# A transformer layer on one core: reordering the first projection, the key and query loads, and the merging of one attention unit

## The chip, the core and the metric

The kernel runs on one core of a Trainium2 chip. The core has a matrix engine (PE; its weight loads are listed apart as PEld), a vector engine (DVE), a scalar engine for activations and copies (ACT), a general engine (POOL), and an engine that issues transfers (SP). Every engine works through its own queue in order and waits on semaphores for the others. The metric is device time in microseconds (us) for one execution; lower is better.

## The reference

Two sequences of 1024 tokens, 512 wide, in float32, go through one post-norm layer. LoRA means that each weight gets half of a rank-16 product added.

```python
q, k, v = (split_heads(lora_linear(x, ...)) for each of q, k, v)      # 16 heads of 32
attn = softmax(q @ k.T * 32 ** -0.5)
x = layernorm(x + lora_linear(merge_heads(attn @ v), Wo, bo, Bo, Ao))
probs = softmax(x @ Wg); expert = argmax(probs); gate = max(probs)    # 8 experts, 256 slots each
routed = gate * ((silu(xe @ W1) * (xe @ W3)) @ W2)                    # 0 for tokens beyond the slots
shared = (silu(x @ sw1) * (x @ sw3)) @ sw2
x = layernorm(x + routed + shared)
```

## The kernel before

Most products are made of two halves. A value is split into a high part, rounded to the fast matrix format, and the low rest; a product is then high·high + low·high + high·low.

**First projection** (lines 216 to 430). Tokens come in four blocks `tb` of 512, weights in four chunks `k` of 128 rows. For block 0 and the query weight the loop at lines 395 to 400 runs over `k`, and `proj_all` (389) calls `proj_k` (306) for each of the four head groups: three matmuls, weight high with token high, weight high with token low, weight low with token high. `split_w` folds the LoRA product into a raw weight chunk (DVE, L284) and splits it (ACT L285 high, DVE L289 low). `split_xk` splits the tokens (ACT L299 high; for block 0 POOL makes the low part, L300). This first part has a written order for ACT, DVE and POOL too; after it only PE's order is written, and a planner places the rest of the projection on the other engines. `split_lora` prepares the LoRA factors of one weight; `prep_w(1, r1)` does it for the key weight after chunk 1. Queries and keys go to DRAM.

**Attention** (lines 587 to 810) has 16 units `u`: one batch, one group `g = u // 2` of four heads, one half of the queries. A unit has 8 steps, one for each block of 128 keys, so step `t = 8u + k`. All engines' orders are written out. In step `t`, `st_step` makes scores for four heads (PE L608) and exponentials (ACT L617) into probability tiles `pt` (two of 128x1024 a step, one for each pair of heads, from a ring of 14). Functions hung into `between[0..3]` run after each of the four heads: `av_step(t-1)` multiplies with the values (PE L635); `adds` sums the probability tiles over the key blocks of a unit; `s1_step` works 12 steps ahead (`LEAD`) on row maxima of a later unit (PE L187, DVE L195), so it ends at step 115; `finish_max` transposes the maxima and hands them to the query tile (`mp`, `mh`, `ml`, L205 to L211).

The sums: POOL adds (L627), except that tile 1 of a unit is added to tile 2 by an accumulating DMA that POOL issues (L655; in unit 13 tiles 1 and 6). In units 14 and 15, DVE and POOL share the adds (`DVE_END`): in unit 14 nine are on DVE and five on POOL, in unit 15 seven and five. `finish(u)` multiplies the sums with ones (PE L670) and, for units 13 to 15, inverts on DVE (L680). `normalize(u)` multiplies (DVE L709), rounds (ACT L711) and takes the rest (DVE L713). In unit 14 it works on unit 13 at its step 7 (t = 119), and in unit 15 on unit 14 at its step 4 (t = 124); `finish(14)` is in step 122.

**Loads.** At `k == 0` of an even unit, SP issues `load_k` for the later half of the next group's keys, three transfers of 256 KB, and `load_q` for unit u+2, three more. `load_k` for the first half is issued at `k == 6` of the odd unit before. `load_res` fetches a residual row block at `RES_AT` (step 8i+6 for the first eight), and POOL adds a bias to it three steps later (`add_res`, L722).

**After it**: the output projection (`oproj`, L739; the first block of batch 1 begins in steps 126 and 127, `OPROJ1`), the list `TAIL`, and the shared experts, 8 blocks `st` of 6 chunks `c`. `SCHED` hangs into (st, c) the preparing of a later block (`p`, transposes), its router logits (`a`: `logits_a`) and their transposition (`b`). `p` and `a` and `b` share two PSUM banks. Then come the router, the scatter and the eight experts.

Of the kernel before, what the change touches and what calls it, by code (L numbers as in the profile page):

```python
# [2 lines left out]

# [10 lines left out]
ALU = mybir.AluOpType  # L14
# [4 lines left out]
P = 128  # L19
B, L, D = 2, 1024, 512  # L20
NU = 16
T = B * L
NH, HD = 16, 32
NG = 4
KC = D // P
# [7 lines left out]
LEAD = 12  # L33
LATE, OP_ONE = (0,), 1
NS = NU * 8
# [21 lines left out]
NRM = 0  # L57
K_AT = 6
XTB = 5
ON_DVE = ()  # L60
ON_DMA = {NU - 3: (1, 6)}
ADDS = {0: (0,), 2: (1,), 3: (3,), 4: (4,), 5: (2,), 6: (5,), 7: (6,)}
ADDS_END = {0: (0,), 2: (1,), 3: (3,), 4: (4,), 5: (2,), 7: (6, 5)}
OPROJ_AT = (65, 67, 69, 71, 73, 75, 77, 79)
RES_AT = tuple(8 * i + 6 for i in range(8)) + (70, 78, 86, 94, 98, 102, 106, 110)
RES_ADDS = tuple(t + 3 for t in RES_AT[:14]) + (118, 119)
RB = 2
BTB = 4
AHEAD = 5
# [1 line left out]
W2_AT = {2: (0, 1), 3: (2, 3), 4: (4,), 5: (5,)}  # L71
MPJ, MPP = 0, 2
RDIR = NU - 3
FINE, NRME = 2, {NU - 2: 7, NU - 1: 4}
DVE_END = {
    NU - 2: ((1, 0), (7, 0)) + tuple((i, 1) for i in range(1, 8)),
    NU - 1: ((1, 0), (2, 0), (3, 0), (4, 0), (5, 0), (6, 0), (6, 1)),
}
OPROJ1 = -2
ROOT_LAG, NORM_LAG = 1, 4  # L80
HSB = 8
TAIL = (
# [3 lines left out]
SCHED = {  # L86
# [4 lines left out]
}  # L91
W13 = 5 * 1024 + 512
# [5 lines left out]
def kernel(  # L98
# [5 lines left out]
    def f(ap):  # L104
        return ap.bitcast(F32)
# [33 lines left out]
    qk_d = {}  # L139
# [4 lines left out]
                    qk_d[w, b, g, hl] = dram.tile([P, L], F32, name=f"qkd{w}{b}{g}{hl}")  # L144
    v_d = [dram.tile([L, D], F32, name=f"vd{b}") for b in range(B)]

    def load_k(g, cs=slice(0, 1024)):
        kt = Ks[g % 2]
        for blk, hl in ((0, 0), (1, 1), (2, 0)):
            sp.dma_start(  # L150
                out=f(kt[32 * blk : 32 * blk + 32, :, cs]),
                in_=qk_d[1, g // NG, g % NG, hl].rearrange("(h p) t -> p h t", p=32)[:, :, cs],
            )

    def load_v(g):
# [8 lines left out]
            ],  # L164
        )

    def load_q(u):
        g, qb = u // 2, u % 2
        for blk, hl in ((0, 0), (1, 0), (2, 1)):
            sp.dma_start(  # L170
                out=f(Qs[u % 3][32 * blk : 32 * blk + 32]),
                in_=qk_d[0, g // NG, g % NG, hl].rearrange("(h p) t -> p h t", p=32)[
                    :, :, qb * 512 : qb * 512 + 512
                ],
            )

# [41 lines left out]
    with ExitStack() as ph1, tc.manual_schedule(engines=MAN1):  # L218
# [33 lines left out]
            return raws  # L252


        def prep_w(i, raws):
            ba = split_lora(i, raws)
            for k, lp in enumerate([fold_w(i, ba, k) for k in range(KC)]):
                split_w(i, k, raws, lp)

        def split_lora(i, raws):  # L260
            ba = []
            for j, lo in ((0, 64), (1, 32)):
                t_ = sg.tile([LR, D], F32R, name=f"lora{i}{j}", tag=f"lora{j}", bufs=1)
                act.copy(t_, raws[j])
                rows = slice(lo, lo + R)
                dve.tensor_tensor(t_[rows], raws[j][rows], f(t_[rows]), ALU.subtract)
                ba.append(t_)
            return ba
# [40 lines left out]
        def proj_k(o, xs, w, g, k):  # L309
            hi, lo = xs[k]  # L310
            a = wh[w][:, k, g * P : g * P + P]
            c = wl[w][:, k, g * P : g * P + P]
            for i, (lhs, rhs) in enumerate(((a, hi), (a, lo), (c, hi))):
                pe.matmul(o, lhs, rhs, start=k + i == 0, stop=k + i == KC + 1)  # L314
# [61 lines left out]
        with tc.manual_schedule(engines=MAN0):  # L376
            dve.memset(bo_bc, 0.0)
            warm("hot", WARM)
            ba = split_lora(0, r0)
            lps = [fold_w(0, ba, k) for k in range(KC)]  # L380
            warm("warm", 1)
            os_ = [bank1(f"o00{g}") for g in range(NG)]
            xs = []

            def split_k(k):
                split_w(0, k, r0, lps[k])
                xs.append(split_xk(0, k, x0[k]))

            def proj_all(k):
                for g in range(NG):  # L390
                    proj_k(os_[g], xs, 0, g, k)

            pool.memset(f(Ks[0][96:98, :, :]), -1.0)
            for k in range(KC):
                split_k(k)
            pool.memset(f(Ks[1][96:98, :, :]), -1.0)
        for k in range(KC):
            proj_all(k)
            if k == KC - 3:
                prep_w(1, r1)  # L400
        for tb in range(4):
            if tb == 0:
                for g in range(NG):
# [23 lines left out]
            xs = xn  # L427
# [161 lines left out]
    with ph2, tc.manual_schedule(engines={mybir.EngineType.PE}):  # L589
# [28 lines left out]
                for fn in between[h]:  # L618
                    fn()

        def add_step(t, pr):
            u, kc = t // 8, t % 8
            if kc == 0:
                accs[u, pr] = pts[t, pr]
            elif kc not in direct(u):
                eng = dve if (kc, pr) in DVE_END.get(u, ON_DVE) else pool
                eng.tensor_tensor(accs[u, pr], accs[u, pr], pts[t, pr], ALU.add)  # L627

        def av_step(t):
            u, kc = t // 8, t % 8  # L630
            g = u // 2
# [9 lines left out]
                    skip_group_check=True,  # L641
                )

        def adds(t):
            u, kc = t // 8, t % 8
            if u in DVE_END:
                for pr in range(2):
                    add_step(t, pr)  # L650
                return
            for j, pr in product((ADDS_END if u in ON_DMA else ADDS).get(kc, ()), range(2)):
                i = u * 8 + j
                if j in ON_DMA.get(u, (1,)):
                    pool.dma_start(out=pts[i + 1, pr], in_=pts[i, pr], accum_op=ALU.add)  # L655
                else:
                    add_step(i, pr)

        def direct(u):
            return () if u in NO_DIR else DIRECT  # L660
# [43 lines left out]
        def normalize(u, parts=(0, 1, 2)):  # L704
            g, qb = u // 2, u % 2
            cs = slice(qb * 512, qb * 512 + 512)
            hi, lo = at_h[:, g % NG, cs], at_l[:, g % NG, cs]
            if 0 in parts:
                dve.tensor_tensor(avs[u], avs[u], fin[u], ALU.mult)  # L709
            if 1 in parts:  # L710
                act.copy(hi, avs[u])  # L711
            if 2 in parts:
                dve.tensor_tensor(lo, avs[u], f(hi), ALU.subtract)  # L713

# [44 lines left out]
        for t in range(NS):  # L759
            u, k = t // 8, t % 8  # L760
            if k == 0:
                if u % 2 == 0 and 2 <= u and u // 2 + 1 < B * NG:
                    load_k(u // 2 + 1, slice(512, 1024))
                if u >= 1 and u + 2 < NU:
                    load_q(u + 2)
                if u % 2 and NG <= u // 2 + 1 < B * NG:
                    load_v(u // 2 + 1)

            if k == K_AT and u % 2 and u // 2 + 2 < B * NG:
                load_k(u // 2 + 2, slice(0, 512))  # L770
            if t in RES_AT:
                load_res(RES_AT.index(t))
            between = [[], [], [], []]
            if t + LEAD < NS:
                for q in range(4):
                    between[q].append(lambda q=q: s1_step(t + LEAD, q))
            elif t + LEAD == NS:
                between[0].append(lambda: finish_max(NU - 1))
            if t:
                between[1].append(lambda: av_step(t - 1))  # L780
                if t == NS - LEAD - 1:

                    between[3].append(lambda: (adds(t - 2), adds(t - 1)))
                elif t != NS - LEAD - 2:
                    between[1].append(lambda: adds(t - 1))
                if u and k == (FINE if u == NU - 1 else FIN):
                    between[1 if u == NU - 1 else FINQ].append(lambda: finish(u - 1))
            if u:
                for v in [u - 2] * (k == NRM and 1 < u < NU - 1) + [u - 1] * (k == NRME.get(u)):
                    between[0].append(lambda v=v: normalize(v, (0,)))  # L790
                    between[1].append(lambda v=v: normalize(v, (1,)))
                    between[2].append(lambda v=v: normalize(v, (2,)))
# [477 lines left out]
```

## Time and profile before

| what | us |
|---|---|
| median of 3 runs (lowest, highest) | 1061.65 (1058.94, 1062.08) |
| the profiled execution | 1072.63 |
| its span, first to last instruction | 1070.8 |

The profiled execution is 10.98 us longer than the median of the runs. Busy time of PE in its stretches, from the view by windows:

| stretch (us) | PE busy (us) | what runs there |
|---|---|---|
| 0 to 60 | 55.55 | first projection, beginning |
| 180 to 250 | 68.15 | attention, first units |
| 450 to 500 | 50.00 | attention |
| 550 to 600 | 45.00 | attention, units 13 to 15 |
| 650 to 700 | 48.81 | shared experts |
| 750 to 800 | 42.66 | router, scatter |
| 900 to 1000 | 100.00 | experts |
| 1000 to 1071 | 58.28 | experts, end |

How to read the views: a group line gives source line, engine, operation, output <- inputs, count, busy time and mean, then the idle time before it and what ended it. A line of the view of waits gives who waited, for whom, the sum in us, how often, and the longest. A timeline line gives start, duration, engine, line, operation and count, and in brackets the idle time before. A line by windows gives for each engine busy time and count, then PE's granted clock, the DMA engines' busy share and GB/s.

### The profile page before, as it was taken

Reading aid. Unit: us, or ns where it says so; the run is one execution under the profiler, and the core shown is the slowest. Engines: PE = TensorE matmul, PEld = TensorE weight load, DVE = VectorE, ACT = ScalarE, POOL = GpSimd, SP = SyncE. Lnnn points to the kernel's source line nnn. Section 1 sums busy time; section 2 is a strip of 40 time slices with the busy share of each in tenths; the row PEclk is TensorE's granted clock in tenths of the full one; section 3 lists DMA queues with packets and bytes.
Section 4 is the critical chain, followed back from the end, with each engine's and each line's share of the span. In section 5 each row is a group of like instructions: output and inputs, shape, how many; then the busy total and the mean of one; then the engine's idle time right before and its main releaser. Section 6 shows DMA issues by size and latency. Waiting matters only on the chain. (4 is left out here: it accounts for less than half of the span.)

```text
span 1070.8 us, 16471 instructions
## 1 busy us (share of the span) xinstructions
PE 1033.8 (97%) x5994; PEld 744.5 (70%) x5994; DVE 697.2 (65%) x1190; ACT 529.2 (49%) x1025; POOL 596.1 (56%) x406
## 2 busy tenths in 40 slices
PE   8999999999999999999998999999979999999995
PEld 6888774444444455544443379899959999999994
DVE  6732788778787877778789974224412567777752
ACT  5422216666666655566665745223102446655552
POOL 4000006999999986979997764000230036766674
PEclk9999999999999999999999999999989999999998
DMA  9876863364637462645643031000280356777721
GB/s 281 280 225 204 250 195 94 78 142 95 143 82 148 115 133 70 131 97 119 143 110 80 1 109 60 21 21 21 92 243 31 118 171 225 254 255 246 258 79 59
DMA packets 84008, 146.68 MB, mean 137 GB/s; under 512 B 14756, under 2 KB 23460, under 8 KB 83928
## 3 DMA queue, kind: packets, MB, share of 16 engines
q1 hardware_dynamic: 75768, 117.30, 37.5%
q0 software_dynamic: 8160, 28.33, 10.7%
q8 instruction: 47, 0.77, 0.3%
q14 instruction: 33, 0.27, 0.1%
HBM read 95.83 MB, written 33.78 MB: 121 GB/s over the span
## 5 line engine op out<-in xcount | busy, mean ns | idle before, releaser
L195 DVE TENSOR_REDUCE mt<-s 128x1 f32<-128x512 f32 x512 | 324.0, 682 | 83.3 <-PE s L187 82.8
L627 POOL TENSOR_TENSOR pt<-pt,pt 128x1024 f32<-128x1024 f32 x148 | 362.0, 2909 | 11.3 <-ACT pt L617 10.8
L617 ACT ACTIVATE pt<-st 128x512 f32<-128x512 f32 x512 | 269.8, 601 | 135.0 <-PE st L608 120.4
L608 PE MATMUL st<-qs,ks 98*128 98x512 f32 x512 | 214.1, 428 | 3.3 <-DVE ml L209 2.1
L187 PE MATMUL s<-ks,qs 96*128 96x512 f32 x512 | 200.3, 398 | 5.3 <-DMA qs<-qkd 4.2
L608 PEld LDWEIGHTS st<-qs,ks 98*128 98x128 f32 x512 | 95.9, 189 | 135.8 <-issue 93.9
L884 PE MATMUL h<-xthe,w13s 128*128 128x256 f32 x704 | 129.9, 283 | 0.0
L872 POOL TENSOR_TENSOR w2s<-w2r,w2s 128x512 fp32r<-128x512 f32 x42 | 65.9, 1590 | 107.4 <-ACT w2s L871 107.2
L655 POOL DMA_DIRECT2D pt<-pt x30 | 27.4, 1078 | 170.5 <-PE st L608 170.5
L187 PEld LDWEIGHTS s<-ks,qs 96*128 96x128 f32 x512 | 97.0, 189 | 26.1 <-DVE mt L195 6.5
L884 PEld LDWEIGHTS h<-xthe,w13s 128*128 128x128 f32 x704 | 110.7, 191 | 0.3
L884 PE MATMUL h<-xtle,w13s 128*128 128x256 f32 x352 | 100.2, 285 | 0.0
L635 PE MATMUL av<-pt,vt 128*32 128x512 f32 x512 | 75.8, 612 | 1.9 <-ACT pt L617 1.9
L1032 POOL DMA_INDIRECT xd_d<-x1a,slot_i x8 | 7.9, 986 | 111.6 <-DVE slot_i L1029 109.5
L635 PE MATMUL av<-pt,x1b 128*32 128x512 f32 x512 | 68.2, 605 | 0.0
L884 PEld LDWEIGHTS h<-xtle,w13s 128*128 128x128 f32 x352 | 67.4, 191 | 0.7
L928 PE MATMUL y<-w2s,hs 128*128 128x512 f32 x260 | 60.9, 390 | 0.1
L928 PEld LDWEIGHTS y<-w2s,hs 128*128 128x128 f32 x260 | 48.2, 188 | 10.2 <-DVE hs L910 0.5
L314 PE MATMUL o<-xh,wh 128*128 128x512 f32 x128 | 50.6, 395 | 1.7 <-ACT xh L299 1.0
L314 PE MATMUL o<-xl,wh 128*128 128x512 f32 x128 | 50.9, 397 | 0.9 <-POOL xl L300 0.9
L329 ACT ACTIVATE oh<-o,bqk_sb 128x512 fp32r<-128x512 f32 x32 | 21.9, 688 | 57.9 <-PE o L314 54.5
L314 PE MATMUL o<-xh,wl 128*128 128x512 f32 x128 | 50.4, 394 | 0.0
(823 smaller groups left out, 1810.9 us busy)
## 6 DMA issues: line engine op xcount, KB each, us to landing
pt<-pt POOLq DMA_DIRECT2D x30, 512.0 KB
qs<-qkd SPq DMA_DIRECT2D x48, 256.0 KB
x1a<-in_w_dram SPq DMA_DIRECT2D x24, 512.0 KB
w2r<-in_w_dram SPq DMA_DIRECT2D x42, 256.0 KB
ks<-qkd SPq DMA_DIRECT2D x36, 256.0 KB
qkd<-oh SPq DMA_DIRECT2D x32, 256.0 KB
qkd<-ol SPq DMA_DIRECT2D x32, 256.0 KB
x1b<-in_w_dram SPq DMA_DIRECT2D x16, 512.0 KB
```

What stands on the lines that cost most here:

```text
L187: pe.matmul(s1, Qs[u % 3][0:96, h, qt * P : qt * P + P], Ks[g % 2][0:96, h, kh * 512 : kh * 512 + 512], start=True, stop=True,)
L195: dve.tensor_reduce(mts[u][:, c, kh : kh + 1], s1, AX.X, ALU.max)
L314: pe.matmul(o, lhs, rhs, start=k + i == 0, stop=k + i == KC + 1)
L329: act.activation(oh, o, AF.Identity, bias=bias)
L608: pe.matmul(sb, Ks[g % 2][:, h, kc * P : kc * P + P], Qs[u % 3][:, h, :], start=True, stop=True,)
L617: act.activation(pts[t, h // 2][:, h % 2, :], sb, AF.Exp, scale=SCALE)
L627: eng.tensor_tensor(accs[u, pr], accs[u, pr], pts[t, pr], ALU.add)
L635: pe.matmul(avs[u][32 * h : 32 * h + 32, :], vts[g][:, kc, 32 * h : 32 * h + 32], pts[t, h // 2][:, h % 2, :], start=kc == 0, stop=kc == 7 ...
L655: pool.dma_start(out=pts[i + 1, pr], in_=pts[i, pr], accum_op=ALU.add)
L872: pool.tensor_tensor(hl[:, 1, :], raw, f(hl[:, 0, :]), ALU.subtract)
L884: pe.matmul(hp[:, j * 256 : j * 256 + 256], lhs, rhs[:, k, :], start=n == 0, stop=n == 11,)
L928: pe.matmul(o, lhs, rhs, start=n == 0, stop=n == 16)
```

## The change

1. The query projection of token block 0: for chunks 0 to 2, four groups with weight high and token high, then four with weight low and token high, then four with token low. `split_lora(1)` is written between the splits of chunk 1 and chunk 2.
2. At `k == 0` of an even unit the three key and three query transfers become two rounds of three and three, each with two of the four heads (128 KB each). Odd units load queries as before.
3. `load_res` of the odd blocks moves to step 8i+2 (and likewise 74 and 90 in the second half; 98 becomes 100), `add_res` three steps later.
4. Unit 14: tiles 0, 2, 4 are added to tiles 1, 3, 5 by DMA (two each, for the two pairs of heads), tiles 3, 6, 7 and 5 to tile 1 by DVE (eight adds), in steps 119 and 120; POOL adds none. Unit 15 keeps its split. `finish(14)` moves to step 123, `normalize(13)` to step 118, `normalize(14)` to step 125, with the rounding and the rest behind the fourth head. For units 13 and 14 the rounding is on DVE instead of ACT.
5. The first block of the output projection of batch 1 no longer begins in steps 126 and 127.
6. `a5` moves from (1, 5) to (2, 0).

```diff
+ADDS = {
+    None: {0: "bb0", 2: "dd1", 3: "pp3", 4: "pp4", 5: "pp2", 6: "pp5", 7: "pp6"},
+    NU - 3: {0: "bb0", 2: "dd1", 3: "pp3", 4: "pp4", 5: "pp2", 7: "dd6 pp5"},
+    NU - 2: {1: "bb1 dd0", 3: "dd2", 5: "dd4", 6: "vv3", 7: "vv6 vv7 vv5"},
+    NU - 1: {0: "bb0", 1: "vp1", 2: "vp2", 3: "vp3", 4: "vp4", 5: "vp5", 6: "vv6"},
+}
-RES_AT = tuple(8 * i + 6 for i in range(8)) + (70, 78, 86, 94, 98, 102, 106, 110)
-RES_ADDS = tuple(t + 3 for t in RES_AT[:14]) + (118, 119)
+RES_AT = tuple(8 * i + (2 if i % 2 else 6) for i in range(8)) + (70, 74, 86, 90, 100, 102, 106, 110)
+RES_ADDS = tuple(t + 3 for t in RES_AT[:14]) + (119, 120)
-FINE, NRME = 2, {NU - 2: 7, NU - 1: 4}
-OPROJ1 = -2
+FINE, NRME = 3, {NU - 2: 6, NU - 1: 5}
+OPROJ1 = 0
+NRM_DVE = (NU - 3, NU - 2)
-    (1, 5): "a5 p6", (2, 1): "b5 a6", (2, 3): "b6", (2, 5): "p7",
+    (1, 5): "p6", (2, 0): "a5", (2, 1): "b5 a6", (2, 3): "b6", (2, 5): "p7",
...
             def proj_all(k):
-                for g in range(NG):
-                    proj_k(os_[g], xs, 0, g, k)
+                hi, lo = xs[k]
+                for i, (w_, x_) in enumerate(((wh, hi), (wl, hi), (wh, lo))):
+                    for g in range(NG):
+                        a = w_[0][:, k, g * P : g * P + P]
+                        pe.matmul(os_[g], a, x_, start=k + i == 0, stop=False)
...
             for k in range(KC):
                 split_k(k)
+                if k == 1:
+                    ba1 = split_lora(1, r1)
...
         def adds(t):
             u, kc = t // 8, t % 8
+            for op in ADDS.get(u, ADDS[None]).get(kc, "").split():
+                i = u * 8 + int(op[2])
                 for pr in range(2):
+                    if op[pr] == "b":
+                        accs[u, pr] = pts[i, pr]
+                    elif op[pr] == "d":
+                        pool.dma_start(out=pts[i + 1, pr], in_=pts[i, pr], accum_op=ALU.add)
+                    else:
+                        eng = dve if op[pr] == "v" else pool
+                        eng.tensor_tensor(accs[u, pr], accs[u, pr], pts[i, pr], ALU.add)
...
             if k == 0:
                 if u % 2 == 0 and 2 <= u and u // 2 + 1 < B * NG:
-                    load_k(u // 2 + 1, slice(512, 1024))
-                if u >= 1 and u + 2 < NU:
+                    for hs in (slice(0, 2), slice(2, 4)):
+                        load_k(u // 2 + 1, slice(512, 1024), hs)
+                        load_q(u + 2, hs)
+                elif u >= 1 and u + 2 < NU:
                     load_q(u + 2)
...
-                if t == NS - LEAD - 1:
-                    between[3].append(lambda: (adds(t - 2), adds(t - 1)))
-                elif t != NS - LEAD - 2:
-                    between[1].append(lambda: adds(t - 1))
+                between[1].append(lambda: adds(t - 1))
```

More of the change, by code (lines that the diff above doesn't have):

```diff
@@ L1 @@
 from contextlib import ExitStack
-from itertools import cycle, product
+from itertools import cycle
 import concourse.bass as bass
@@ L59 @@
 XTB = 5
[L60 to L63, printed above, removed]
+ADDS = {
[4 more added lines that the diff above has]
+}
 OPROJ_AT = (65, 67, 69, 71, 73, 75, 77, 79)
-RES_AT = tuple(8 * i + 6 for i in range(8)) + (70, 78, 86, 94, 98, 102, 106, 110)
-RES_ADDS = tuple(t + 3 for t in RES_AT[:14]) + (118, 119)
+RES_AT = tuple(8 * i + (2 if i % 2 else 6) for i in range(8)) + (70, 74, 86, 90, 100, 102, 106, 110)
+RES_ADDS = tuple(t + 3 for t in RES_AT[:14]) + (119, 120)
 RB = 2
@@ L73 @@
 RDIR = NU - 3
-FINE, NRME = 2, {NU - 2: 7, NU - 1: 4}
[L75 to L78, printed above, removed]
-OPROJ1 = -2
+FINE, NRME = 3, {NU - 2: 6, NU - 1: 5}
+OPROJ1 = 0
+NRM_DVE = (NU - 3, NU - 2)
 ROOT_LAG, NORM_LAG = 1, 4
@@ L145, with load_k @@
     v_d = [dram.tile([L, D], F32, name=f"vd{b}") for b in range(B)]
-    def load_k(g, cs=slice(0, 1024)):
+    def load_k(g, cs=slice(0, 1024), hs=slice(0, 4)):
         kt = Ks[g % 2]
@@ L150, in load_k @@
             sp.dma_start(
-                out=f(kt[32 * blk : 32 * blk + 32, :, cs]),
-                in_=qk_d[1, g // NG, g % NG, hl].rearrange("(h p) t -> p h t", p=32)[:, :, cs],
+                out=f(kt[32 * blk : 32 * blk + 32, hs, cs]),
+                in_=qk_d[1, g // NG, g % NG, hl].rearrange("(h p) t -> p h t", p=32)[:, hs, cs],
             )
@@ L165, in load_v, with load_q @@
         )
-    def load_q(u):
+    def load_q(u, hs=slice(0, 4)):
         g, qb = u // 2, u % 2
@@ L170, in load_q @@
             sp.dma_start(
-                out=f(Qs[u % 3][32 * blk : 32 * blk + 32]),
+                out=f(Qs[u % 3][32 * blk : 32 * blk + 32, hs]),
                 in_=qk_d[0, g // NG, g % NG, hl].rearrange("(h p) t -> p h t", p=32)[
-                    :, :, qb * 512 : qb * 512 + 512
+                    :, hs, qb * 512 : qb * 512 + 512
                 ],
@@ L252, in load_w, with prep_w @@
             return raws
-        def prep_w(i, raws):
-            ba = split_lora(i, raws)
+        def prep_w(i, raws, ba=None):
+            ba = ba or split_lora(i, raws)
             for k, lp in enumerate([fold_w(i, ba, k) for k in range(KC)]):
@@ L395 @@
                 split_k(k)
+                if k == 1:
+                    ba1 = split_lora(1, r1)
             pool.memset(f(Ks[1][96:98, :, :]), -1.0)
         for k in range(KC):
-            proj_all(k)
+            if k < KC - 1:
+                proj_all(k)
+            else:
+                for g in range(NG):
+                    proj_k(os_[g], xs, 0, g, k)
             if k == KC - 3:
-                prep_w(1, r1)
+                prep_w(1, r1, ba1)
         for tb in range(4):
@@ L619, in st_step @@
                     fn()
[L621 to L627, printed above, removed]
         def av_step(t):
@@ L647, in adds @@
             u, kc = t // 8, t % 8
-            if u in DVE_END:
+            for op in ADDS.get(u, ADDS[None]).get(kc, "").split():
+                i = u * 8 + int(op[2])
                 for pr in range(2):
[L650 to L657, printed above, removed]
+                    if op[pr] == "b":
+                        accs[u, pr] = pts[i, pr]
+                    elif op[pr] == "d":
+                        pool.dma_start(out=pts[i + 1, pr], in_=pts[i, pr], accum_op=ALU.add)
+                    else:
+                        eng = dve if op[pr] == "v" else pool
+                        eng.tensor_tensor(accs[u, pr], accs[u, pr], pts[i, pr], ALU.add)
         def direct(u):
@@ L710, in normalize @@
             if 1 in parts:
-                act.copy(hi, avs[u])
+                if u in NRM_DVE:
+                    dve.tensor_copy(hi, avs[u])
+                else:
+                    act.copy(hi, avs[u])
             if 2 in parts:
@@ L788 @@
             if u:
[L789 to L792, printed above, removed]
+                if k == NRM and 1 < u < NU - 1:
+                    for q in range(3):
+                        between[q].append(lambda q=q: normalize(u - 2, (q,)))
+                if k == NRME.get(u):
+                    for q in range(3):
+                        between[(0, 3, 3)[q]].append(lambda q=q: normalize(u - 1, (q,)))
             if t in RES_ADDS:
```

## The prediction, made before the changed kernel was seen

> **What bounds the kernel now.** I read the page's busy line first, then PE's waits, then the timeline around each wait.
>
> ```profile
> PE 1033.8 (97%) x5994; PEld 744.5 (70%) x5994; DVE 697.2 (65%) x1190; ACT 529.2 (49%) x1025; POOL 596.1 (56%) x406
> ```
>
> PE is busy for 97% of the span, so 1070.8 - 1033.8 = 37 us are all that taking waits away can give, apart from matmuls stretched by a slow clock or by waiting operands. PE's waits over the whole span say whose:
>
> ```profile
> PE s L187 <- DMA qs<-qkd: 4.2, 4, 1.5
> PE h-1_5_1_7907 L884 <- issue: 3.9, 6, 1.6
> PE y-1_4_0_7938 L928 <- issue: 3.3, 3, 2.0
> PE st L608 <- DVE ml L209: 2.1, 1, 2.1
> PE av L635 <- ACT pt L617: 1.9, 1, 1.9
> ...
> PE tps L452 <- ACT ls L511: 1.1, 2, 0.8
> ...
> PE o L314 <- POOL xl L300: 0.9, 1, 0.9
> PE o L314 <- DVE ol L330: 0.8, 1, 0.8
> ```
>
> The change aims at lines 1, 4, 5, 6 and the last two. The two "issue" lines lie at 776 to 790 us, beside the scatter, and stay; so does the drain of some 12 us at the end.
>
> **Loads by head pairs, and the residual moved** (changes 2, 3). The four waits of 4.2 us lie at 225, 279, 334 and 519 us, each in an even unit as the first row-maximum matmul wants its queries. SP's timeline before the first:
>
> ```profile
> 210.46 1.32 SPq L150 DMA_DIRECT2D ks<-qkd  x3
> 211.82 0.43 SPq L718 DMA_DIRECT2D x1a<-in_x_dram  x1
> 212.35 1.33 SPq L150 DMA_DIRECT2D ks<-qkd  x3
> 213.72 2.88 SPq L170 DMA_DIRECT2D qs<-qkd  x3
> ```
>
> Ten transfers of 256 KB, 2.6 MB, stand in one bunch, and the needed one is last. The windows 216 to 222 us show the DMA engines' share at 1.07 and 1.08 and 223 to 225 GB/s: the bunch is bound by the engines. After the change, heads 0 and 1 wait for 3 x 256 + 6 x 128 KB = 1.57 MB; 1.05 MB less at 224 GB/s is 4.7 us earlier, against a longest wait of 1.5. Heads 2 and 3 are first used four row-maximum steps later (12 us). SP issues six instructions more (0.44 us each, 2.6 us); behind them on SP stands only the store of the sums at k = 4, at 229.58, long after. Here a rule speaks against the change: the Trainium skill, "DMA: Bandwidth & Descriptors", sections "Anatomy of one DMA" and "Rules for kernel authors", gives each DMA about 2 us fixed and asks for 1 MiB. If twelve of 128 KB paid 2.3 us one after the other (an estimate from that page), the sixth would land 13.8 us after the first was issued, just at the need: no gain. But in this trace several fly at once and their sum is bandwidth, so I take the row: 4.2 us, of which 0.4 is left for waits that merely shrink, **3.8 us** (ends 2.5 and 4.2).
>
> What gets worse is POOL. Odd units now hold two residual adds (1.7 us each), even ones none. POOL needs 52.4 us for two units (from the first accumulating DMA at 170.55 to that at 222.96, without idle), PE 2 x 26.64 = 53.3 without waits: 0.9 us of cover a pair. In an odd unit the last add ends 1.7 us later; the sums are needed about 4.5 us after it now. Cost 0; without that cover, up to 1 us a pair.
>
> **Unit 14** (changes 4, 5). The timeline of DVE, ACT and POOL:
>
> ```profile
> 573.06 5.66 DVE L627 TENSOR_TENSOR pt<-pt,pt 128x1024 f32<-128x1024 f32 x3
> 578.65 0.27 DVE L209 TENSOR_TENSOR ml<-mp,mh 16x128 fp32r<-16x128 f32 x1
> ...
> 593.84 3.78 DVE L627 TENSOR_TENSOR pt<-pt,pt 128x1024 f32<-128x1024 f32 x3
> ...
> 605.31 2.80 DVE L627 TENSOR_TENSOR pt<-pt,pt 128x1024 f32<-128x1024 f32 x1
> 608.03 0.68 DVE L713 TENSOR_TENSOR at_l<-av,at_h 128x512 fp32r<-128x512 f32 x1
> 608.63 8.60 DVE L627 TENSOR_TENSOR pt<-pt,pt 128x1024 f32<-128x1024 f32 x4
> ...
> 590.68 0.59 ACT L711 CAST at_h<-av 128x512 fp32r<-128x512 f32 x1 [2.96 <-DVE av L709]
> ...
> 601.32 2.38 POOL L627 TENSOR_TENSOR pt<-pt,pt 128x1024 f32<-128x1024 f32 x1 [1.27 <-ACT pt L617]
> 603.97 9.71 POOL L627 TENSOR_TENSOR pt<-pt,pt 128x1024 f32<-128x1024 f32 x3 [0.27 <-ACT pt L617]
> ```
>
> Three adds stand ahead of `ml` on DVE, and PE waits 2.1 us for the bank that `ml` frees; ACT's rounding waits 2.96 us for a DVE product behind adds, with the exponentials behind it. Steps here take 2.65 us undisturbed, 5.5 around that rounding. But removing both is not worth its sum, because DVE is the last to arrive: it works nearly without pause from 573 to 617.23, and the sum of unit 15 ends at 618.26 only because of it. So I add up DVE's new queue. A DVE add takes 3.78/3 = 1.26 us while POOL rests (593.84), 2.8 to 3.2 beside a POOL add.
>
> Without adds `ml` is done at 574; the ones-product of unit 13 ends at 576.4. Reciprocal 3.36 us (row L680), product 0.69, rounding on DVE (nearest row L713, 0.68), rest 0.68: 581.8. Eight adds with POOL at rest, 8 x 1.26 = 10.1: 591.9. PE reaches `finish(14)` at 576.3 + 7 x 2.65 = about 594.9, so it doesn't wait; cover 3 us. Then unit 15: four adds beside POOL at 3.0, reciprocal 3.36, product, rounding and rest 2.05, three adds at 1.26: 21.2, DVE ends at **613.1**, 4.1 us before 617.23. The Trainium skill ("SBUF — State Buffer", section "The single rule") calls the port that a two-input DVE add shares with POOL an exclusive lock. Then a pair would take 2.38 + 1.26 = 3.64 instead of 3.0, and the end would be 615.7; the measured pairs (2.80 beside 9.71/3 = 3.24) overlap more, so I take them. From the 4.1 us goes the output block that now runs wholly behind the sums: six matmuls of 0.23, 1.4 us. PE will wait about 2.5 us for DVE near 610; after the 2.1 us wait at 577 the clock was granted at 0.50 (window 580 to 582), so I take 0.5 us for a slow restart. **2.2 us**; ends -9.6 (third rival) and 4.5.
>
> The six new DMAs are issued by a resting POOL (1.1 us each). A pair issued at 170.5 was through by about 177.5, 7 us; here the pairs start near 570, 575 and 580, and are wanted at 582 (two of them) and 589.4. Cover 0 to 2 us on DVE, backed by the 3 us before `finish(14)`. Tile buffers come free in that order too.
>
> **Start** (change 1). PE waits 0.9 us for the first low tokens; behind that the windows 9 to 13 us show the clock at 0.63, 0.50, 0.50, 0.66. On ACT the key weight's LoRA factors stand ahead of chunk 1 and wait for their transfer until 10.25, though chunk 1 could be rounded at 9.1. Afterwards chunk 1 is whole at 11.6 instead of 14; the LoRA casts (1.3 us ACT, 1.4 DVE) lie in a wait. PE, at half clock from 9.3 to 12.6 as now, ends chunk 3 at 21.7 instead of 23.05; never slowed, at 20.2. But the next product waits for DVE's `ol`, until 23.99 now, and DVE is busy 1.9 of every 2 us from 20 to 28 in an order that the planner chooses. Ends 0 and 3.7; I take **1.2**, nearer to the end where DVE stays in the way.
>
> **Logits** (change 6). At 693 to 695 us eight logit matmuls and the transposes of block 6 share two banks; the second transposes wait 0.82 us for ACT's copy. Alone, neither waits: **0.8 us** (0.5 to 0.9).
>
> **Sum**: 3.8 + 2.2 + 1.2 + 0.8 = 8.0 us, from 1072.63 to 1064.6 for the profiled execution. The runs lie 10.98 us below it, and the stalls counted are in other places than the scatter; I subtract from the median: 1061.65 - 8.0 = **1053.7**.
>
> **Rivals.** *First (0.17):* only loads and logits come through; the start stays behind `ol`, and DVE's end moves only by what the output block gives back. 4.6 us, 1057.0. For it: DVE's full queues at both places. *Second (0.13):* the start keeps full clock and DVE keeps up: 3.7 instead of 1.2, and no slow restart: 11.5 us, 1050. *Third (0.10), slower:* DVE alone is too slow for unit 14. If its adds there cost 2.8 us (port taken by descriptor work or the DMAs), eight end at 604.2, PE waits some 9 us in `finish(14)`, DVE ends at 625.4; with the output block 9.6 us lost, 5.8 won, 1065.4. It decides from 2.3 us an add. Against it: 1.26 with POOL at rest.
>
> **Numbers.** The likeliest case has 0.60, with 1050 to 1057 as its own range. The four cases and the runs' scatter give 1048 to 1061. 0.3% is 3.2 us, about what a measurement of this kernel can tell from no change. Faster by more: nearly all of the likeliest and the second rival and half of the first, 0.81; same 0.11; slower 0.08.
>
> **What would show it.** Right: no wait of L187 on qs above 0.5 us; DVE adds in 582 to 592 at about 1.3 us; the last DVE add near 613; no wait of L452 at (1, 5). Wrong: a wait of L670 on DVE near 595; DVE adds above 2 us; accumulating DMAs landing after 590; L187 waiting for DVE or ACT for POOL in place of the load; PE back at the key projection no earlier than 24 us.

## The result and the profile after

| kernel, chip | before (us, median) | changed (us, median) | ratio, 95% interval |
|---|---|---|---|
| changed kernel, first chip, 14 runs | 1060.78 | 1054.47 (1051.64 to 1058.68) | 0.9951 [0.9934, 0.9968] |
| the same, second chip, 8 runs | 1062.55 | 1055.76 (1051.77 to 1058.75) | 0.9941 [0.9918, 0.9965] |

The changed kernel is faster: the ratios say 5.2 us [3.4, 7.0] and 6.3 us [3.7, 8.7] (the medians in the table lie 6.3 and 6.8 us apart), where the forecast's sum was 8.0. The median on the first chip is 0.8 us above the predicted 1053.7. It would have been farther off if the forecast had started from before's median over 14 runs, which lies 0.9 us below that of the three runs shown.

The two profiled executions don't compare by their spans (1070.8 and 1056.1). Before's has 11 us at the scatter that after's has not: from the last scatter transfer to the last `y` matmul it takes 271.9 us in before, 260.8 in after. Kernels of this study that ran on a third chip, where before's median was 1074.03, have 271 to 272 us there too, and PE waits of 5.5 to 7.2 us on "issue" (7.2 in before, none in after). So those 11 us go with the chip or the occasion, not with the change. I compare milestones ahead of that place.

| milestone (us) | before | after | won so far |
|---|---|---|---|
| first matmul of the key projection | 23.99 | 21.54 | 2.4 |
| first row-maximum matmul | 114.6 | 112.2 | 2.4 |
| last row-maximum `mx` (DVE) | 572.9 | 566.5 | 6.4 |
| last matmul of the output projection | 641.4 | 640.1 | 1.3 |
| last transposition of the logits | 740.1 | 737.8 | 2.3 |

`mx` is the last step of the row maxima, and the times further below are counted from it. Start and loads won 6.4 us up to there, and the end of attention gave back 5.1 of it. The busy line of the page after:

```profile
PE 1030.1 (98%) x5994; PEld 742.5 (70%) x5994; DVE 696.0 (66%) x1191; ACT 527.1 (50%) x1023; POOL 585.9 (55%) x407
```

PE's waits in after, over the whole span:

```profile
PE sm L672 <- DVE pt L659: 6.9, 3, 4.7
...
PE s L189 <- DVE mt L197: 1.0, 3, 0.3
...
```

The waits of the row-maximum matmul (now L189) for its queries are gone, all 4.2 us. So are those for `ml` and for the exponentials in unit 14. At the head stands a new one: the ones-product of `finish` (L672) waits for DVE's sums, 6.9 us. SP's timeline in after, where before had ten transfers of 256 KB in one bunch:

```profile
207.89 2.73 SPq L152 DMA_DIRECT2D ks<-qkd  x6
210.66 1.36 SPq L172 DMA_DIRECT2D qs<-qkd  x3
212.76 1.92 SPq L152 DMA_DIRECT2D ks<-qkd  x3
214.94 1.31 SPq L172 DMA_DIRECT2D qs<-qkd  x3
```

The first six key transfers are three of 256 KB and three of 128. The queries of heads 0 and 1 come behind them and heads 2 and 3 last. The last of the twelve small transfers landed at 219.83, 11.9 us after the first issue of the bunch; from 210 to 218 us the DMA engines moved 239 to 257 GB/s, where the bunch of before had 220 to 226 (216 to 222 us). Now the end of attention in after, the timelines of DVE, POOL and PE:

```profile
575.64 1.22 DVE L659 TENSOR_TENSOR pt<-pt,pt 128x1024 f32<-128x1024 f32 x1
579.23 16.86 DVE L659 TENSOR_TENSOR pt<-pt,pt 128x1024 f32<-128x1024 f32 x9 [2.37 <-DMA pt<-pt]
...
604.85 7.78 DVE L659 TENSOR_TENSOR pt<-pt,pt 128x1024 f32<-128x1024 f32 x3
...
568.88 1.75 POOL L656 DMA_DIRECT2D pt<-pt  x2 [4.88 <-PE av L639]
...
585.14 6.55 POOL L659 TENSOR_TENSOR pt<-pt,pt 128x1024 f32<-128x1024 f32 x2 [5.84 <-ACT pt L629]
592.26 8.53 POOL L659 TENSOR_TENSOR pt<-pt,pt 128x1024 f32<-128x1024 f32 x3 [0.56 <-ACT pt L629]
605.30 2.96 POOL L568 TENSOR_TENSOR w13s-1_0_6235<-w13r,w13s-1_0_6235 128x1024 fp32r<-128x1024 f32 x1 [4.51 <-ACT w13s-1_0_6235 L562]
608.23 3.32 POOL L568 TENSOR_TENSOR w13s-1_1_6240<-w13r,w13s-1_1_6240 128x1024 fp32r<-128x1024 f32 x1
...
609.40 1.40 PE L672 MATMUL sm<-pt,ones 128*32 128x512 f32 x4 [4.67 <-DVE pt L659]
612.68 1.92 PE L672 MATMUL sm<-pt,ones 128*32 128x512 f32 x4 [1.88 <-DVE pt L659]
```

Three things are to be seen. POOL could issue the second pair of accumulating DMAs only at 568.88, when PE had read the tiles that it writes, and DVE waits 2.37 us for the second transfer of that pair. Of DVE's adds, six from 579.23 on follow each other every 1.14 us (each takes 1.22); from 585 on they meet POOL's adds of unit 15 and take 3.2 to 3.4. And ACT, which no longer waits, is through by 602.8, so POOL splits the shared expert's first weights (L568) just beside DVE's last two adds: the three take 7.78 us. PE stands still for 6.5 us between, and its granted clock, the third number from the end of a line by windows, is at 0.50 from 610 to 616 us:

```profile
610.00:612.00 2.00, 0.80 (x4) 0.00 (x0) 2.00 (x1) 0.00 (x0) 1.92 (x4) 0.50 0.52 209
```

On the first chip the runs of the changed kernel fall into two groups: nine of 1051.6 to 1055.5 us and five of 1057.6 to 1058.7. On the second chip its eight runs spread over the same range, without two clear groups. The profiled execution (1057.8) is of the later group; an early one (1051.9) was profiled on the second chip (below).

### The profile page after: what moved, and what is told of

It is laid out like the page before. It is cut to its first block, busy times and chain, and to the rows that moved or that the text cites. A ratio compares the mean times of both kernels' runs of the same rounds, so it can differ in the third digit from the quotient of the medians.

```text
span 1056.1 us, 16556 instructions
## 1 busy us (share of the span) xinstructions
PE 1030.1 (98%) x5994; PEld 742.5 (70%) x5994; DVE 696.0 (66%) x1191; ACT 527.1 (50%) x1023; POOL 585.9 (55%) x407
## 5 line engine op out<-in xcount | busy, mean ns | idle before, releaser
L659 POOL TENSOR_TENSOR pt<-pt,pt 128x1024 f32<-128x1024 f32 x143 | 350.7, 2918 | 6.7 <-ACT pt L629 6.4
L189 PE MATMUL s<-ks,qs 96*128 96x512 f32 x512 | 200.3, 398 | 1.0 <-DVE mt L197 1.0
L656 POOL DMA_DIRECT2D pt<-pt x36 | 33.3, 1113 | 174.4 <-PE st L620 165.0
L189 PEld LDWEIGHTS s<-ks,qs 96*128 96x128 f32 x512 | 97.1, 190 | 20.3 <-DVE mt L197 5.6
L934 PEld LDWEIGHTS y<-w2s,hs 128*128 128x128 f32 x260 | 48.2, 188 | 10.2 <-DVE hs L916 0.5
L316 PE MATMUL o<-xh,wh 128*128 128x512 f32 x116 | 45.5, 392 | 0.3 <-DVE ol L332 0.3
L901 ACT ACTIVATE sl<-h 128x256 f32<-128x256 f32 x40 | 15.4, 385 | 60.5 <-PE h L890 59.2
L316 PE MATMUL o<-xh,wl 128*128 128x512 f32 x116 | 45.4, 391 | 0.0
```

The lines of the kernel that those rows point to most:

```text
L189: pe.matmul(s1, Qs[u % 3][0:96, h, qt * P : qt * P + P], Ks[g % 2][0:96, h, kh * 512 : kh * 512 + 512], start=True, stop=True,)
L659: eng.tensor_tensor(accs[u, pr], accs[u, pr], pts[i, pr], ALU.add)
L934: pe.matmul(o, lhs, rhs, start=n == 0, stop=n == 16)
```

## The experiments

Times are ratios to before on the same chip, over five rounds of runs each; traces are of one execution each.

**The whole change again, and its parts.** The changed kernel once more, without an edit:

> The changed kernel once more, beside the parts on one chip. My theory: 0.995 of before, about 6 us less. If the early batch's chip differed, another ratio comes here, and the parts have to be compared with that one.

Ratio 0.9941 [0.9918, 0.9965], as expected. Its execution took 1051.9 us, 5.9 less than the one above, with the same program. DVE, POOL and PE in it, and one of its windows:

```profile
576.62 18.35 DVE L659 TENSOR_TENSOR pt<-pt,pt 128x1024 f32<-128x1024 f32 x10 [1.12 <-DMA pt<-pt]
...
603.88 4.55 DVE L659 TENSOR_TENSOR pt<-pt,pt 128x1024 f32<-128x1024 f32 x3
...
576.15 2.98 POOL L727 TENSOR_TENSOR x1b<-x1b,bo_bc 128x512 f32<-128x512 f32 x2
...
595.31 2.35 POOL L659 TENSOR_TENSOR pt<-pt,pt 128x1024 f32<-128x1024 f32 x1 [3.88 <-ACT pt L629]
...
609.46 2.40 POOL L568 TENSOR_TENSOR w13s-1_0_6235<-w13r,w13s-1_0_6235 128x1024 fp32r<-128x1024 f32 x1 [4.58 <-ACT w13s-1_0_6235 L562]
...
592.56 1.05 PE L672 MATMUL sm<-pt,ones 128*32 128x512 f32 x4 [2.23 <-DVE pt L659]
...
594.00:596.00 2.00, 2.00 (x11) 0.70 (x10) 2.00 (x2) 1.92 (x4) 0.69 (x1) 0.54 0.00 0
...
```

Here the first transfer of the second DMA pair landed 10.2 us after `mx` instead of 9.0. DVE's first add began beside POOL's residual adds (576.15) and took 3.6 us, and the second add came at 580.14 instead of 579.23. With that lag two adds of unit 14, not one, met POOL's first adds of unit 15; PE waited 2.23 us for unit 14's sum, and its clock fell to 0.54 and 0.60 (594 to 598 us). In this execution that wait is a gain: ACT's exponentials come some 4 us later, POOL's adds thin out, its splits start at 609.46, after DVE's last add, and the three last adds take 4.55 us. The last projection matmul comes 67.9 us after `mx`, against 73.6.

So the end of attention takes one of two courses, 6 us apart. The traces below show where they part. POOL has no adds of unit 14 any more, and in all eight traces of kernels with these sums its residual adds begin 9.8 us after `mx` (before: 13.8 and 19.3). In the first trace alone DVE's first add began early enough, 9.1 us after `mx`, to take 1.2 us. In the seven others it began at 9.4 to 10.4 and took 3.5 to 4.5, and the second add came at 13.8 instead of 12.7. Five of the seven then took the better course; the other two have a later ones-product (below). **In these traces a quarter of a microsecond in the landing of a DMA lies between the two courses.**

Edits 2 and 3 alone, on the kernel before:

```diff
-                    load_k(u // 2 + 1, slice(512, 1024))
-                if u >= 1 and u + 2 < NU:
+                    for hs in (slice(0, 2), slice(2, 4)):
+                        load_k(u // 2 + 1, slice(512, 1024), hs)
+                        load_q(u + 2, hs)
+                elif u >= 1 and u + 2 < NU:
...
```

> The kernel before with keys and queries loaded by head pairs and the residual loads moved, nothing else. My theory: the four waits of PE L187 on the queries (4.2 us together) go and nothing takes their place: the last row-maximum matmul comes about 4 us earlier and the time falls by 3 to 4 us (ratio 0.9965). The rival that what is won is eaten at the end of attention, because DVE's full queue in unit 14 ends at the same time after mx: the stretch keeps its length, so 4 us stay. The rival of a fixed price for each small transfer: the queries land no sooner, the waits stay, ratio 1.000.

Ratio 0.9968 [0.9952, 0.9984], 3.4 us [1.7, 5.1] less, and no wait for queries is left. The rule of a fixed price for each small transfer is out. In the profiled execution (the longest of its ten runs, 1061.0) `mx` came 3.2 us earlier, but the last projection matmul only 0.3. PE's waits there between `mx` and that matmul:

```profile
PE av L635 <- ACT pt L617: 4.2, 1, 4.2
PE st L608 <- DVE ml L209: 2.1, 1, 2.1
```

The first was 1.9 in before. Two things made it longer. The clock stayed at 1.00 after the wait for `ml`, where it had fallen to 0.50 in before, so PE came 1.3 us sooner. And DVE's product for the rounding was done 1.1 us later: the residual adds now come a step later, POOL puts an add of unit 14 ahead of them, and DVE's add beside it took 3.18 us instead of 2.12. Behind the longer wait the clock was at 0.50 from 588.6 to 595.4. No run moved the residual adds alone, so what they cost in other executions is open. The rival that DVE eats the gain holds for that execution and not for the median.

Edit 1 alone, on the kernel before:

```diff
-                for g in range(NG):
-                    proj_k(os_[g], xs, 0, g, k)
+                hi, lo = xs[k]
+                for i, (w_, x_) in enumerate(((wh, hi), (wl, hi), (wh, lo))):
+                    for g in range(NG):
+                        a = w_[0][:, k, g * P : g * P + P]
+                        pe.matmul(os_[g], a, x_, start=k + i == 0, stop=False)
...
+                if k == 1:
+                    ba1 = split_lora(1, r1)
...
```

> The kernel before with the first projection's low half last and the LoRA factors' split moved, nothing else. My theory from the trace of the changed kernel: key projection begins 2.4 us earlier (21.5 for 24.0) and the gain is carried through to the end, 2 to 2.5 us, ratio 0.998. The rival from my forecast: DVE's ol holds the next product, 1.2 us or less, ratio 0.999 to 1.000.

Ratio 0.9997 [0.9985, 1.0010]: alone it is worth nothing that can be measured, and the trace of one execution shows why, in a way that neither theory had. Attention does begin 2.3 us earlier (112.3), but its last `mx` comes 1.6 us later (574.5). PE's largest wait in attention:

```profile
PE s L187 <- DMA qs<-qkd: 3.4, 3, 2.0
```

The windows at its longest case, first one of before and then those of this run:

```profile
334.00:336.00 2.00, 2.00 (x17) 0.70 (x20) 1.29 (x2) 0.60 (x1) 2.00 (x2) 1.00 1.04 201
...
330.00:332.00 2.00, 0.12 (x1) 0.00 (x0) 0.93 (x3) 0.86 (x2) 2.00 (x3) 0.95 0.81 171
332.00:334.00 2.00, 1.89 (x7) 1.03 (x11) 0.93 (x2) 0.60 (x1) 2.00 (x2) 0.50 1.15 223
...
336.00:338.00 2.00, 2.00 (x16) 0.39 (x8) 0.00 (x0) 0.00 (x0) 2.00 (x1) 0.50 0.00 0
```

The load's wait in unit 6 was 1.2 us in before, with the clock at 1.00 after it; here it is 2.0, and PE runs at half clock for some 6.6 us, by estimate 3.3 us of work. Where edit 2 has taken the waits away, edit 1 pays: in the next run, which has both, `mx` comes 1.9 us earlier than with the loads alone.

**Unit 14 as before**, everything else changed (the residual adds stay where edit 3 put them):

```diff
-    NU - 2: {1: "bb1 dd0", 3: "dd2", 5: "dd4", 6: "vv3", 7: "vv6 vv7 vv5"},
+    NU - 2: {0: "bb0", 1: "vv1", 2: "pv2", 3: "pv3", 4: "pv4", 5: "pv5", 6: "pv6", 7: "vv7"},
...
-FINE, NRME = 3, {NU - 2: 6, NU - 1: 5}
-OPROJ1 = 0
-NRM_DVE = (NU - 3, NU - 2)
+FINE, NRME = 2, {NU - 2: 7, NU - 1: 4}
+OPROJ1 = -2
+NRM_DVE = ()
...
```

> The changed kernel with unit 14 as before (nine adds on DVE, five on POOL, old steps of finish and normalize, rounding on ACT, output block begun in steps 126 and 127); start, loads and logits stay changed. Theory A (the unit 14 edit lost time: in the profiles the stretch from the last row maxima to the end of the first output block grew from 46.8 to 52.0 us): about 5 us faster than the changed kernel's 1054.5, so 1049.5, and that stretch again near 47 us. Theory B (the edit gained its forecast 2.2 us in the runs, and the longer stretch is one execution's or is made good later): 1056.7.

Ratio 0.9940 [0.9919, 0.9960], not to be told from the whole change: a loss of 5 us by unit 14 is out, and a gain of 2.2 is not seen either. And with only the rounding of units 13 and 14 on DVE (`NRM_DVE` kept, the rest of this edit as above):

> The changed kernel with the sums of unit 14, the output block and the order of the pieces as before; only the rounding of the normalized h of units 13 and 14 stays on DVE. Theory (the sums' place on DVE and POOL bounds, the rounding only stalls ACT ahead of time): PE's wait of 4.2 us for the exponentials goes or shrinks under 1 us, DVE's last add still ends near 616, and the time is that of the kernel with all of unit 14 as before, 1056 to 1057, ratio 0.994 to 0.995. Rival (the stalls themselves were the loss): the last projection matmul comes 3 us or more earlier, 1053, ratio 0.991.

Ratio 0.9943 [0.9922, 0.9965]. PE's wait of 4.2 us did not go; its name changed:

```profile
PE av L639 <- DVE at_l L718: 4.3, 1, 4.3
...
```

PE waits for the bank that the normalize of unit 13 reads, so for DVE's queue, not for ACT. The time is what I had expected, the reason not; the last projection matmul comes 69.6 us after `mx`, 1.9 sooner than with all of unit 14 as before (71.5), less than the rival's 3.

**The output block begun early again**, in the changed kernel:

```diff
-OPROJ1 = 0
+OPROJ1 = -2
```

> The changed kernel with the first output block begun in steps 126 and 127 again. Theory A: its first six matmuls lie in PE's wait for DVE's last adds; 1.4 us, and up to 1 us more if PE's shorter idling leaves the clock at full, so 1052 to 1053. Rival (the block waits for unit 14's rest on DVE at 605 us and holds up steps 126 and 127 with it, so the last exponentials and with them the last adds come later): no gain or up to 3 us slower.

Ratio 0.9916 [0.9892, 0.9940] over six runs. Its profiled execution took the better course, and there its last projection matmul (67.8 us after `mx`) is where the changed kernel's is on that course (67.9).

**POOL's splits behind DVE's last adds**, by two orders of the tail; the second leaves the router's set-up, `w0`, ahead of the splits:

```diff
-    "l0 l1 t0 s0 s1 n1 n2 w0 o1 o2
+    "l0 l1 t0 n1 n2 s0 s1 w0 o1 o2
```

```diff
-    "l0 l1 t0 s0 s1 n1 n2 w0 o1 o2
+    "l0 l1 t0 n1 n2 w0 s0 s1 o1 o2
```

> The changed kernel with the first two weight splits of the shared experts (s0, s1) behind the rounding and the rest of unit 15 in TAIL. Theory A (POOL's two splits at 605 to 611 us, early because ACT ran dry, stretch DVE's last two adds from 1.25 to 3.1 and 3.4 us): the last two adds at 1.25 us each, DVE done 4 us sooner, time 1050.5. Rival (POOL's splits are themselves wanted by the shared experts, or the adds are slow for another reason): adds still near 3 us, or PE waits for the weights later, time within 1 us of 1054.5.

> The changed kernel with the last normalize pieces and the router's set-up ahead of the two weight splits in the tail's order. Theory (the splits on POOL beside DVE's last adds and the router weight's load behind the weights' loads are both in the way): the last three adds of unit 15 take about 4.5 us together instead of 7.8, ACT waits for the router's weight under 1 us, and the end comes 2 to 4 us before the changed kernel's (ratio 0.991 to 0.993). Rival (PE idles because the output block has been moved behind the sums, whatever POOL does): PE still waits 4 us or more for DVE's adds and the ratio stays at 0.995 to 0.997.

The first gave 0.9967 [0.9955, 0.9979]: the collision went (last three adds 4.55 us), but the router's weight now landed behind the shared expert's weights, DVE waited 8.2 us behind it and PE 3.2 (the last projection matmul 73.7 us after `mx`). The second, with that repaired, gave 0.9930 [0.9914, 0.9946], its six runs within 1053.1 to 1055.4, so none in the late group. That agrees with the theory in the time; but PE's wait of 2.2 us at 590 is in its profile too, so it doesn't show that the order alone made it.

**DVE's wait for the second DMA pair taken away**: the sums of that pair are DVE's own, two adds more:

```diff
-    NU - 2: {1: "bb1 dd0", 3: "dd2", 5: "dd4", 6: "vv3", 7: "vv6 vv7 vv5"},
+    NU - 2: {1: "dd0", 2: "bb2", 3: "vv3", 5: "dd4", 6: "vv1", 7: "vv6 vv7 vv5"},
```

> The changed kernel with other sums in unit 14: DMA adds tile 0 to 1 and 4 to 5 only; DVE adds tile 3 to tile 2 at step 116, where it idled 2.4 us ahead of the ones-product, then 1, 6, 7, 5: ten adds on DVE, four DMAs instead of six. Theory A (DVE idled 2.4 us for the second pair of accumulating DMAs, which landed 9.7 us after its issue): no wait of DVE for a DMA, the last add of unit 14 about 2.8 us sooner relative to the row maxima, at most that much faster: 1052. Rival (the port and the adds of unit 15 set the end anyhow, or the reciprocal of unit 13 is pushed back by the adds ahead of it): no gain, up to 2 us slower.

Ratio 0.9982 [0.9970, 0.9993], slower than the changed kernel. DVE's timeline in it:

```profile
576.46 20.44 DVE L659 TENSOR_TENSOR pt<-pt,pt 128x1024 f32<-128x1024 f32 x10
...
605.65 7.78 DVE L659 TENSOR_TENSOR pt<-pt,pt 128x1024 f32<-128x1024 f32 x3
```

No wait for the DMA is left, but the adds, now 17, took 34.2 us in all. Unit 14's sum was done 22.9 us after `mx`, PE waited only 0.3 us for it, and the execution took the late course (three last adds 7.78 us, last projection matmul 73.1 us after `mx`). None of its 22 runs is below 1058.3. So taking that wait away alone doesn't help.

**The ones-product of unit 14 a step later**, and its normalize too, with the tail as in the changed kernel, and with `w0` ahead of the splits:

```diff
-FINE, NRME = 3, {NU - 2: 6, NU - 1: 5}
+FINE, NRME = 4, {NU - 2: 6, NU - 1: 6}
```

> The changed kernel with the ones-product of unit 14 one step later (and its normalize one step later), nothing else. In three of four profiled executions so far PE waited 2.2 us there for DVE's last add of unit 14, and the steps behind it, at half clock, came later. Theory (DVE bounds the stretch; the wait there does no harm, because it keeps ACT and so POOL's weight splits away from DVE's last adds): the wait near 590 us goes, but the last scores come by 602 instead of 606, POOL's splits meet DVE's last adds in every execution, PE waits over 4 us before the last ones-product, and the time is that of the changed kernel's late executions, 1057 to 1058 (ratio 0.996). Rival (the wait in the ones-product is what the unit lacks against the forecast): the time falls by 2 us or more, to 1053 or less, ratio 0.992.

> The same later ones-product together with the tail's order in which the router's set-up and the last normalize pieces stand ahead of the weight splits, so that POOL has no split beside DVE's last adds. Theory (DVE bounds the stretch): the last three adds take 4.5 us together, PE's wait only moves from 590 to before the last ones-product, and the time is that of the changed order alone, 1052.5 to 1054 (ratio 0.993). Rival as above: the removed wait adds to it, 1051 or less.

They ran on the third chip: 0.9955 [0.9939, 0.9971] and 0.9953 [0.9937, 0.9970]. The traces are plain. In the first, PE's waits between `mx` and the last projection matmul:

```profile
PE sm L672 <- DVE pt L659: 7.5, 2, 6.6
...
```

The wait at 590 shrank to 0.9 us, the last scores came 4 us earlier than on the better course, and the end 75.6 us after `mx`: the worst of all, as the theory had it. But the second ended late too (72.7), with no split beside the last adds. So POOL's splits are not the whole cause. When PE runs through at 590, POOL's adds of unit 15 follow each other closely and meet DVE's adds of units 14 and 15 one after the other. Side by side, in us, all but the second column of numbers counted from `mx`:

| kernel | last scores | busy in DVE's adds | DVE's last add ends | last projection matmul |
|---|---|---|---|---|
| before | 41.0 | | 44.3 | 68.5 |
| loads alone | 44.0 | | 47.4 | 71.6 |
| unit 14 as before | 44.0 | | 47.3 | 71.5 |
| changed, 1051.9 us execution | 39.2 | 26.7 | 42.0 | 67.9 |
| output block early | 40.6 | 27.8 | 42.2 | 67.8 |
| tail with `w0` ahead | 40.4 | 28.5 | 43.1 | 69.0 |
| changed, 1057.8 us execution | 35.0 | 29.5 | 46.1 | 73.6 |
| `FINE` 4, `w0` ahead | 35.5 | 30.3 | 45.8 | 72.7 |
| `FINE` 4 | 35.6 | 33.5 | 48.2 | 75.6 |

The upper three do 16 other adds. The lower six do the same 15; alone, at 1.22 us each, they would take 18.3. Of these, the three that are busy for 29.5 us and more end at 45.8 to 48.2 and the other three at 42.0 to 43.1: where the adds overlap more with POOL's work, DVE ends later, and PE, which reached its last scores some 5 us earlier, waits for it. **Both repairs together** (output block early, `w0` ahead):

> The changed kernel with both repairs: the output block begun ahead of the last sums again, and the tail's order with the splits last. If each removes a cause of its own, the two add up: 1051 or less (ratio 0.990). If both remove the same thing (POOL's splits beside the last adds, PE at rest before the last ones-product), no more than the better of them: 1052 to 1053.5, ratio 0.991 to 0.993, with all runs within about 2 us of each other.

Ratio 0.9947 [0.9930, 0.9964] on the third chip, 68.7 us from `mx`, runs spread over 7 us. They don't add up, and the intervals of these last three, of unit 14 with the rounding alone and of the changed kernel overlap. The two variants with ratios of 0.9916 and 0.9930 lie below the changed kernel's medians, but I can't call either of them better: the first's advantage was not repeated in combination, and the second's rests on six runs beside eight of the changed kernel on one chip, with intervals that overlap.

## Why the prediction held, point by point

**Loads: held.** Forecast 3.8; no wait for queries is left, attention is 4.0 us shorter in the trace (6.4 less the start's 2.4), and alone the change is worth 3.4 us [1.7, 5.1]. Twelve small transfers beside three large ones landed within 11.9 us; by the estimate of 2.3 us for each, one after the other, the twelve would have taken 27.6. So the row was the better guide. That estimate took the price for one of every DMA; the section that it names, "Anatomy of one DMA" in the Trainium skill's "DMA: Bandwidth & Descriptors", gives it for DMAs that POOL issues, and these are issued by SP.

**Start: mis-sized.** Forecast 1.2, with 3.7 if DVE's `ol` were not in the way. Key projection began 2.4 us earlier, for `ol` itself was done at 21.5 instead of 23.9: DVE was not in the way as I had feared. The half clock at 9 to 13 us, which the forecast kept, is absent after (1.00 from 5.8 us on), but that isn't what won: the loads alone have full clock there too and begin the row maxima at 114.5, against 114.6 before. That the start is worth this only behind the loads' change I did not see: I added terms that are not independent.

**Logits: held.** Forecast 0.8; the wait fell from 1.1 to 0.3.

**Unit 14: mis-sized.** Forecast 2.2; between the whole change and the one without it no difference can be measured. The traces give the stretch behind `mx` 3.6 us shorter on one course and 2.1 longer on the other (67.9 and 73.6 against 71.5); before, with its residual adds a step earlier than those 71.5, had 68.5. PE reached the ones-product of unit 14 about where I had put it: 22.0 us after `mx` by the forecast, 21.6 and 22.9 in the traces. The term that failed is "Eight adds with POOL at rest, 8 x 1.26 = 10.1": I had them end 19.0 us after `mx`; they ended 22.9 and 26.1 after it. They began about when I had thought (9.1 and 10.3 us after `mx`, forecast 8.9), but POOL was not at rest. Its residual adds lay beside the first of them in the second trace, which took 3.6, and its adds of unit 15 began at 585, where one or two of the eight took 3.4. The wait for the second DMA pair, which I had covered by "0 to 2 us on DVE", took 2.4 in the first trace. So the 3 us of cover were gone, and "The last DVE add near 613" came true in the profile (612.6) only because `mx` itself was 6.4 us earlier; counted from `mx` I had 40.2, the traces have 42.0 and 46.1. For a pair beside POOL I had 3.0, against the 3.64 of an exclusive port; DVE's adds took 3.2 to 3.4 and POOL's 3.24, between the two.

The output block cost more than 1.4 plus 0.5 us on the late course: twelve matmuls from 614.5 to 618.6, the first at half clock. On the better course it cost nothing that can be seen.

**Luck.** That the median came within 0.8 us is in part luck: the start won 1.2 us more than its term, unit 14 about 2.2 less, and the median that the sum was taken from was 0.9 too high.

**The rivals.** The third, slower one asked for 2.8 us an add; uncontended adds took 1.22, with accumulating DMAs still in flight (the last landed at 584.15). The first comes nearest in what it says: loads and logits, and an end of DVE that moves by nothing that lasts; but the start gave 2.4 us to it that it denied. The second's sum was wrong: 2.5 and 0.5 more than 8.0 are 11.0, not 11.5.

Left open: why the runs of one kernel land now on one course, now on the other. Two edits took PE's wait at 590 away or nearly so (the second pair's sums on DVE, and the later ones-product), and all three of their traces end late, so that wait belongs to the better course. What shifts the landing of the DMA from one execution to the next was not found, and no experiment forced the landing itself.

## What to carry to other kernels

Gains from removed waits are not independent: a stage that begins earlier can lengthen the next stage's wait for a load, and a longer wait can cost clock besides, so take the downstream wait away first and then the upstream one. Where two engines slow each other down, add up how many of their instructions will lie side by side after the change, counted from the same milestone and with every instruction that the change itself moves there, rather than the price of one alone. And where the time of a changed kernel has two groups, profile more than one execution before explaining either.

## What the runs showed of the hardware

The granted clock fell to half after waits of PE of 2.0 us (332 us, edit 1 alone) and 2.2 us (592.6 us, the changed kernel's second trace), and stayed at 1.00 after one of 1.2 us at the first of these places in before. The length of a wait alone does not decide it. PE's wait of 2.1 us for `ml` was followed by half clock in before (first line) and by full clock in the loads alone (second line):

```profile
580.00:582.00 2.00, 2.00 (x9) 0.20 (x8) 2.00 (x2) 1.13 (x3) 1.92 (x2) 0.50 0.61 113
576.00:578.00 2.00, 2.00 (x12) 0.61 (x11) 2.00 (x1) 1.58 (x3) 1.92 (x2) 1.00 0.31 49
```

The Trainium skill ("TensorE: Matmul & The Clock Gate", section "What's actually happening") puts the drop after at least one idle window of about 3.4 us; here 2.0 us was enough in one place and 2.1 was not in another. The drop after the wait of 2.0 us cost by estimate 3.3 us more (6.6 us at half clock).

A DVE add of 128x1024 took 1.22 us alone (in a row one began every 1.14) and 3.2 to 3.4 beside a POOL add, which itself went from 2.35 to 3.24. An added wait of 2.2 us on PE went with an execution 6 us shorter, in which the adds of the two engines lay farther apart.
